# A four-layer hybrid on one core: Mamba's weights and the first group statistics made during layer 0, later norms on ACT, bias tables by chunk

## The chip, the core and the metric

The kernel is one program on 1 core of one Trainium2 chip. Its time is device microseconds of one execution. Five runs of the kernel before took 7926.34 to 7949.28 us, with a median of 7930.91 us. Engines are named as in the profile: PE multiplies matrices (PEld is its weight load), DVE is the vector engine, ACT the scalar engine, POOL the general one, and SP issues the DMAs.

## The reference, cut to what matters

Four images of 56 x 56 positions and 128 channels pass through four layers. Each layer adds its result to x.

```python
def _gn(v, G=32, eps=1e-5): ...     # group norm over all positions and 4 channels of each group

x = x + _L0_conv_ref(_gn(x), ...)   # attention of 4 heads in a 7 x 7 neighbourhood, with a bias
                                    # rpb[head, rel_row, rel_col], softmax, projection
x = x + _L1_conv_ref(_gn(x), ...)   # two Mamba blocks along each row of 56 positions

def _mamba_block(h, in_w, cw, cb, xw, dtw, dtb, A_log, Dp, ow):
    u, res = split(h @ in_w)
    u = silu(causal_conv(u, cw) + cb)          # 4 taps
    dt, Bm, Cm = split(u @ xw)
    delta = softplus(dt @ dtw + dtb)
    A = -exp(A_log)                            # 256 channels x 16 states
    y = selective_scan(u, delta, A, Bm, Cm) + u * Dp
    return y * silu(res) @ ow
```

Layers 2 and 3 (additive attention, experts, softmax attention, a router) are not touched by the change. All is float32.

## The kernel before

x stays in SBUF as four tiles X (112 rows of two image lines, 28 tiles of 128 channels). The work of an image is cut into 7 chunks of 448 positions (8 image lines). On PE, ACT, DVE and POOL the order of instructions in layers 0 to 2 is the order in which the code calls them; the order of SP's DMAs is set by a scheduler, and each DMA of SP also waits until the DMA eight before it is done.

**Group norm** (`group_norm_steps`, L167 to L238). `transposed(c)` turns four tiles of a chunk on PE into a PSUM tile m (L179). `taken(c)` takes its statistics on DVE (`bn_stats`, L190) and copies the chunk unnormed into xnT on ACT (L191), which waits for the statistics; at chunk 0 POOL sets the pad to zero (L188). Six steps follow: aggregate on DVE (L195), mean over the group by a matmul (L199), deviations (L203 to L207), another matmul, variance and ACT's Sqrt (L211, L213), its inverse (L218 to L222). Last, `normed` subtracts the mean and multiplies on DVE in place (L226), seven instructions for an image, called in groups of 2, 2 and 3 chunks. `group_norm_coarse` joins these into twelve steps for layer 0.

**Bias tables** (`bias_tables`, L249 to L300). A table of exp(bias) is made from a constant `toep` (14 x 3136) and the transposed rpb: seven matmuls (L272) and seven ACT exponentials (L276) into one SBUF tile tab, one DMA to a DRAM tile dtab (L279), and 56 DMAs from there into e_edge (42, L285) and e_inner (14, L295), by which the weights of attention are multiplied.

**Layer 0** (`layer0`). SP's order at the start, in the program as built, is: toep, four of rpbT, image 0 in two halves, group, wqkv, bqkv, wproj, bproj, image 1's first half, dtab, image 1's second half, the 56 table DMAs, images 2 and 3. PE's order is: the seven table matmuls, image 0's norm, the first queries, keys and values, scores of the first two units. A chunk is four units, 112 in all. In unit i PE makes the scores of the unit after next (L440) and sums (L470), ACT the exponentials (L450), DVE (three heads) and POOL (one head) the products with the tables (L455); then come the steps that a dictionary `at` holds for this unit: queries (L403, L405), keys, values, the parts of `finish` (copies L485, reciprocal L490, product L491, projection L496, sum into X L499). The twelve norm steps of image b + 1 are spread over units 0 to 16 of image b, so image 3 has none. Layer 0's PSUM pool for m has two buffers.

**Layer 1** (`layer1_weights`, `layer1`, `mamba_pre`). When layer 0 has ended, the weights are loaded and worked: taps times in_proj (L604), A times a pick matrix (L607), D times a unit matrix (L613), columns of x_proj (L601), exp(A_log) on ACT (L596). Then image 0's group norm is done at one go, and the loop over pairs starts. There are 56 blocks (image, chunk, Mamba layer) of 16 pairs. A pair is two matmuls to decays (L671) and inputs (L680), an exponential E on ACT (L696), a product with the inputs on DVE (L701), a scan on DVE (L708) and a product on POOL (L713); PE sums them (L719). The dictionaries `first` and `last` hold what else is done in a pair, before and after its scan: the block's preparation (`mamba_pre`: convolution L826, silu L838, projections L844 and L855, softplus L869, residual L880) one block ahead, and, in the last five blocks before an image starts, that image's transposes, statistics and norms. Layer 1's PSUM pool for m has one buffer.

Of the kernel before, what the change touches and what calls it, by code (L numbers as in the profile page):

```python
# [2 lines left out]

# [16 lines left out]
P = 128  # L20
# [84 lines left out]
class Hybrid:  # L105
# [61 lines left out]
    def group_norm_steps(self, b, pool, psum, group, pad=0):  # L167

        nc = self.nc
        got = {}
        chunk = lambda c: got["xn"][:, c * SEQ : (c + 1) * SEQ, pad:]

        def transposed(c):
            got["ps"] = ps = psum()
            for k in range(TC):
                nc.tensor.transpose(  # L179
                    ps[:, k * TP : (k + 1) * TP], self.X[b][:, TC * c + k, :], self.ident[:TP, :TP]  # L180
                )

        def taken(c):
            if c == 0:
                got["xn"] = self.t(pool, [P, HW, pad + HW], "xnT")
                got["st"] = self.t(pool, [P, NCH, nc.vector.BN_STATS_DIM], "gn_st")
                if pad:
                    nc.gpsimd.memset(got["xn"][:, :, 0:pad], 0.0)  # L188
            ps = got["ps"]
            nc.vector.bn_stats(got["st"][:, c, :], ps[:, :CH])  # L190
            nc.scalar.copy(chunk(c), ps[:, :CH].rearrange("p (s t) -> p s t", t=HW))  # L191

        def aggregate():
            got["mv"] = self.t(pool, [P, 2], "gn_mv")
            nc.vector.bn_aggr(got["mv"], got["st"])  # L195

        def by_group(of):
            got["ps"] = psum()
            nc.tensor.matmul(got["ps"][:, 0:1], group, of(), start=True, stop=True)  # L199

        def mean():
            got["mean"] = mean = self.t(pool, [P, 1], "gn_mean")
            nc.vector.tensor_copy(mean, got["ps"][:, 0:1])  # L203
            got["dev"] = dev = self.t(pool, [P, 1], "gn_dev")
            nc.vector.tensor_sub(dev, got["mv"][:, 0:1], mean)
            nc.vector.tensor_mul(dev, dev, dev)
            nc.vector.tensor_add(dev, dev, got["mv"][:, 1:2])  # L207

        def var():
            got["ve"] = ve = self.t(pool, [P, 1], "gn_ve")  # L210
            nc.vector.tensor_scalar(ve, got["ps"][:, 0:1], 1e-5, None, op0=ALU.add)  # L211
            got["r"] = self.t(pool, [P, 1], "gn_r")
            nc.scalar.activation(got["r"], ve, AF.Sqrt)  # L213

        def root():
            r, ve = got["r"], got["ve"]
            q = self.t(pool, [P, 1], "gn_q")
            nc.vector.reciprocal(r, r)  # L218
            nc.vector.tensor_mul(q, r, r)
            nc.vector.tensor_mul(q, q, ve)  # L220
            nc.vector.tensor_scalar(q, q, -0.5, 1.5, op0=ALU.mult, op1=ALU.add)
            nc.vector.tensor_mul(r, r, q)  # L222

        def normed(cs):
            for c in cs:
                nc.vector.tensor_scalar(  # L226
                    chunk(c), chunk(c), got["mean"], got["r"], op0=ALU.subtract, op1=ALU.mult
                )

        bind = lambda f, c: lambda: f(c)  # L230
        return got, (
            [(bind(transposed, c), bind(taken, c)) for c in range(NCH)],
            [
                aggregate, lambda: by_group(lambda: got["mv"][:, 0:1]), mean,
                lambda: by_group(lambda: got["dev"]), var, root,
            ],
            [bind(normed, cs) for cs in (range(0, 2), range(2, 4), range(4, NCH))],
        )  # L238

    def group_norm_coarse(self, *args):  # L240

        got, (chunks, stats, norms) = self.group_norm_steps(*args)
        both = lambda fs: lambda: [f() for f in fs]
        return got, [both(fs) for fs in chunks] + [both(stats[:3]), both(stats[3:])] + norms
# [4 lines left out]
    def bias_tables(self, pool, tmp, dr, m):  # L249
# [9 lines left out]
        toep = self.load(tmp, [1 + KR, S], "toep", a["k_toep"])  # L259
# [8 lines left out]
        def make():  # L268
            tab = self.t(tmp, [NH * KR, S], "tab")
            for c in range(NCH):  # L270
                ps = m()[: NH * KR]
                nc.tensor.matmul(  # L272
                    ps[:, :CH], rT.rearrange("p h r -> p (h r)"), toep[:, c * CH : (c + 1) * CH],
                    start=True, stop=True,
                )
                nc.scalar.activation(tab[:, c * CH : (c + 1) * CH], ps[:, :CH], AF.Exp)  # L276

            dtab = dr.tile([NH, KR, HW, HW], F32, name="dtab")
            nc.sync.dma_start(out=dtab.rearrange("h r k j -> (h r) (k j)"), in_=tab)  # L279
# [70 lines left out]
    def layer0(self):  # L350
# [5 lines left out]
        with ExitStack() as ctx:  # L356
# [20 lines left out]
            bproj = self.load(wp, [TP, C], "bproj", a["L0_conv_b_proj"].partition_broadcast(TP))  # L377
            for b in range(1, B):
                self.load_image(b)
# [8 lines left out]
            def norm_steps(b):  # L388
                got, steps = self.group_norm_coarse(b, big, m, group)

                def hand_over():
                    steps[-1]()
                    xn[b] = got["xn"].rearrange("p i j -> p (i j)")

                return steps[:-1] + [hand_over]
# [125 lines left out]
            for k, (b, c) in enumerate(chunks):  # L521
# [9 lines left out]
                if c == 0 and b + 1 < B:  # L531
                    for n, step in enumerate(norm_steps(b + 1)):
                        add(i + 3 * n // 2, step)
            scores(0)
# [15 lines left out]
    def layer1_weights(self, wp):  # L550
        nc, a = self.nc, self.a
        w = {}
# [32 lines left out]
        with ExitStack() as ctx:  # L585
            tmp = ctx.enter_context(self.tc.tile_pool(name="l1_tmp", bufs=1))
            iw = self.load(tmp, [P, NL, DI], "iw", in_w[:, :, 0:DI])
            cw = self.t(tmp, [P, NL, DI, DC], "cw")
            nc.sync.dma_start(
                out=cw.rearrange("p l f k -> p (l f k)"),  # L590
                in_=a["L1_conv_conv_w"].rearrange("l f o k -> (l f o k)").partition_broadcast(P),
            )
            A = self.load(
                tmp, [P, NL, NHALF, DS], "A", by_channel("L1_conv_A_log", "l (h p) n -> p l h n")
            )
            nc.scalar.activation(A, A, AF.Exp)  # L596
            xw = self.load(
                tmp, [P, NL, NHALF, DBL], "xw_in", by_channel("L1_conv_x_proj_w", "l (h p) k -> p l h k")
            )
            for at, n, src in ((0, DR, 0), (HD, DR, 0), (2 * HD, DS, DR), (3 * HD, DS, DR + DS)):  # L600
                nc.vector.tensor_copy(w["xw"][:, :, :, at : at + n], xw[:, :, :, src : src + n])  # L601
            for l in range(NL):
                for k in range(DC):
                    nc.vector.tensor_mul(w["in"][:, l, k, :], iw[:, l, :], cw[:, l, :, k])  # L604
                for f in range(NHALF):
                    for q in range(QG):
                        nc.vector.scalar_tensor_tensor(  # L607
                            w["A"][:, l, f, q, :].rearrange("p (j n) -> p j n", n=DS),
                            w["pick"][:, q, :].rearrange("p (j n) -> p j n", n=DS), -1.0,
                            A[:, l, f, :].unsqueeze(1).to_broadcast([P, P // DS, DS]),  # L610
                            op0=ALU.mult, op1=ALU.mult,
                        )
                    nc.vector.tensor_scalar(  # L613
                        w["Dd"][:, l, f, :], self.ident, w["D"][:, l, f : f + 1], None, op0=ALU.mult
                    )
        return w

    def layer1(self):
# [5 lines left out]
        with ExitStack() as ctx:  # L624
            wp = ctx.enter_context(tc.tile_pool(name="l1_w", bufs=1))
            w = self.layer1_weights(wp)
# [21 lines left out]
            def prepare_image(b):  # L648

                got, (chunks, stats, norms) = self.group_norm_steps(b, big, m, w["group"], DC - 1)  # L650

                def hand_over():
                    for c in range(NCH):
                        h[b, c, 0] = got["xn"][:, c * SEQ : (c + 1) * SEQ, :]

                return chunks, stats, norms + [hand_over]
# [117 lines left out]
            for j, block in enumerate(order):  # L774
                at = PAIRS * j
                if j and block[1:] == (0, 0):

                    chunks, stats, norms = prepare_image(block[0])
                    for k, (turn, take) in enumerate(chunks):
                        to = at - (5 - k // 3) * PAIRS + 11 + k % 3  # L780
                        add(last, to, turn)
                        add(first, to + 1, take)
                    to = at - 3 * PAIRS + 12
                    for k, (where, step) in enumerate(zip((first, last) * 3, stats)):
                        add(where, to + k // 2, step)
                    for k, step in enumerate(norms):
# [1038 lines left out]
```

## Time and profile before

| what | us |
|---|---|
| median of five runs | 7930.91 |
| the profiled execution (the slowest of the five) | 7949.28 |
| its span in the profile | 7947.5 |
| busy PE, DVE, ACT, POOL | 6744.0, 6087.7, 5019.8, 2552.0 |
| the start, up to the first product with a bias table (L455) | 42.06 |
| last instruction of layer 0 (L499) starts | 563.64 |
| first convolution of layer 1 (L826) starts | 603.39 |
| first scan of layer 1 (L708) starts | 638.34 |

Times in rows of the timeline count from the span's start. A row has start, duration, engine, line, operation, what it writes and reads, how many, and in brackets how long the engine stood idle before it and what ended that. SPq rows are the issues of DMAs, not the transfers. A table by stage has, after the length, busy time and count of PE, PEld, DVE, ACT and POOL, then the mean granted clock of PE, the share of DMA and GB/s. A row of a line's or group's view has count, and least, median and longest duration in ns.

### The profile page before, as it was taken

The page shows a single profiled execution, that of the slowest core. Times are in us where ns is not written, and L with a number is a line of the kernel's source. Part 1 is how long each engine was busy: PE and PEld are TensorE (multiplying, and loading weights), DVE is VectorE, ACT ScalarE, POOL GpSimd, SP SyncE. Part 2 cuts the span into 40 slices and gives each one's busy share as a digit, 9 for nine tenths or more (in the row PEclk, how much of TensorE's full clock was granted, in tenths as well). Part 3 has the DMA queues.
Part 4 walks back from the last instruction along what each step waited for, and adds up shares of the span by engine and source line. Part 5 has one row for each costly group of instructions (what it writes and reads, how often), then busy time and mean ns, then how long its engine had stood idle before and what let it go on. Part 6 is the DMA issues. An engine that isn't in the chain of part 4 may idle for free.

```text
span 7947.5 us, 105809 instructions
## 1 busy us (share of the span) xinstructions
PE 6744.0 (85%) x41037; PEld 2683.2 (34%) x41037; DVE 6087.7 (77%) x10253; ACT 5019.8 (63%) x4916; POOL 2552.0 (32%) x1909
## 2 busy tenths in 40 slices
PE   8878998998999899977777777777777889999999
PEld 4442333333333333322222222222222344444544
DVE  6777999999999999986877886887787755344434
ACT  4545555555555555537998899899889964333332
POOL 4545776777777677750000000000001000000000
PEclk9989999999999999988999999899899989999999
DMA  2000000000000000000000000000003101210000
GB/s 54 2 14 1 1 1 1 1 1 1 1 1 1 1 1 1 1 5 1 1 1 1 5 1 1 1 5 1 1 28 116 46 6 40 96 56 5 6 5 6
DMA packets 85490, 102.36 MB, mean 13 GB/s; under 512 B 21158, under 2 KB 50742, under 8 KB 84279
## 3 DMA queue, kind: packets, MB, share of 16 engines
q1 hardware_dynamic: 84985, 95.58, 4.1%
q8 instruction: 322, 5.28, 0.3%
q14 instruction: 183, 1.50, 0.1%
HBM read 85.28 MB, written 10.29 MB: 12 GB/s over the span
## 4 chain that ended last, share of the span: by engine, by line
DVE 36%; PE 35%; ACT 20%; issue 7%; POOL 1%; DVEq 0%; DMA 0%; SPq 0%; ACTq 0%; POOLq 0%
DVE hs L708 17%; ACT th L1051 13%; DVE u L701 7%; PE q L1597 7%; PE o L1608 7%; PE s L1062 6%; DVE th L1042 5%; PE o L1089 3%; PE pe L1762 2%; ACT E L696 2%; DVE e L455 2%; PE a L671 2%; PE m L826 1%; DVE d L490 1%; ACT e L450 1%
## 5 line engine op out<-in xcount | busy, mean ns | idle before, releaser
L1051 ACT ACTIVATE th<-th 128x3136 f32<-128x3136 f32 (+12 forms) x1120 | 2294.2, 2093 | 209.2 <-DVE th L1042 155.5
L1042 DVE TENSOR_SCALAR th<-fT,g 128x784 f32<-128x784 f32 (+6 forms) x3920 | 1917.0, 555 | 504.1 <-PE s L1062 467.7
L713 POOL TENSOR_TENSOR hs<-hs,bc 128x896 f32<-128x896 f32 x896 | 1868.2, 2085 | 798.8 <-DVE hs L708 770.6
L1062 PE MATMUL s<-th,place 128*32 128x392 f32 (+8 forms) x14336 | 1497.5, 495 | 668.5 <-ACT th L1051 665.4
L708 DVE TENSOR_TENSOR_SCAN hs<-E,u 128x896 f32<-128x896 f32 x896 | 1809.3, 2019 | 115.7 <-DVE u L701 2.0
L696 ACT ACTIVATE E<-a 128x896 f32<-128x896 f32 x896 | 821.5, 917 | 812.5 <-PE u L680 342.7
L671 PE MATMUL a<-delta,A_pick 32*128 32x448 f32 x3584 | 984.2, 601 | 147.0 <-ACT E L696 138.9
L680 PE MATMUL u<-du,pick 32*128 32x448 f32 x3584 | 981.5, 603 | 47.5 <-DVE hs L708 47.4
L701 DVE TENSOR_TENSOR u<-u,bc 128x896 f32<-128x896 f32 x896 | 963.6, 1075 | 47.2 <-PE u L680 46.9
L1062 PEld LDWEIGHTS s<-th,place 128*32 128x32 f32 (+1 forms) x14336 | 429.3, 111 | 1616.1 <-ACT th L1051 1083.9
L1602 ACT ACTIVATE e<-q,shift 128x448 f32<-128x448 f32 (+1 forms) x700 | 440.7, 633 | 733.1 <-PE q L1597 732.8
L1080 POOL TENSOR_TENSOR e<-e,later 112x112 f32<-112x112 f32 x112 | 80.1, 715 | 2337.7 <-ACT e L1073 1688.5
L1608 PE MATMUL o<-e,xk 128*128 128x448 f32 (+1 forms) x1400 | 654.6, 550 | 25.6 <-ACT oT L1583 25.6
L1767 DVE SCALAR_TENSOR_TENSOR X<-pe,r_gate,X 112x128 f32<-112x128 f32 x896 | 313.8, 350 | 456.2 <-PE pe L1762 420.7
L1597 PE MATMUL q<-xT 128*128 128x448 f32 (+1 forms) x1400 | 655.5, 550 | 6.0 <-ACT e L1602 5.9
L671 PEld LDWEIGHTS a<-delta,A_pick 32*128 32x128 f32 x3584 | 296.2, 188 | 694.7 <-ACT E L696 465.4
L719 PE MATMUL y<-hs,sum 128*32 128x448 f32 x3584 | 445.2, 568 | 4.4 <-POOL hs L713 4.4
L1089 PE MATMUL o<-e,xa 112*128 112x392 f32 (+5 forms) x1024 | 438.8, 552 | 1.1 <-POOL e L1080 1.1
L680 PEld LDWEIGHTS u<-du,pick 32*128 32x128 f32 x3584 | 297.4, 189 | 213.9 <-DVE hs L708 196.1
L1608 PEld LDWEIGHTS o<-e,xk 128*128 128x128 f32 (+1 forms) x1400 | 263.0, 192 | 310.4 <-issue 275.5
L1597 PEld LDWEIGHTS q<-xT 128*128 128x128 f32 (+1 forms) x1400 | 249.1, 190 | 244.0 <-issue 212.1
L1696 POOL MEMSET lc_xa<- 112x4 f32 x28 | 3.1, 109 | 894.8 <-DVE lc_xa L1690 580.1
(251 smaller groups left out, 7226.2 us busy)
## 6 DMA issues: line engine op xcount, KB each, us to landing
wide<-in_L_ffn_weight SPq DMA_DIRECT2D x64, 1024.0 KB
X<-in_x SPq DMA_DIRECT2D x8, 784.0 KB
out<-X SPq DMA_DIRECT2D x28, 224.0 KB
M<-wide SPq DMA_DIRECT2D x4, 784.0 KB
wide<-M SPq DMA_DIRECT2D x4, 784.0 KB
e_edge<-dtab SPq DMA_DIRECT2D x42, 49.0 KB
cw<-in_L_conv_conv_w SPq DMA_DIRECT2D x1, 1024.0 KB
c_h<-in_L_ffn_weight SPq DMA_DIRECT2D x16, 64.0 KB
```

The lines of the kernel that those rows point to most:

```text
L671: nc.tensor.matmul(halves(to)[:, k], w["A"][own, order[j][2], f, q, :], pre[j]["delta"][own, f], start=True, stop=True,)
L680: nc.tensor.matmul(halves(to)[:, k], w["pick"][own, q, :], pre[j]["du"][own, f], start=True, stop=True,)
L696: nc.scalar.activation(E[p + 1], t, AF.Exp)
L701: nc.vector.tensor_mul(v, v, pre[p // PAIRS]["bc"][:, 0:1].to_broadcast([P, 2, CH]))
L708: nc.vector.tensor_tensor_scan(flat, E.pop(p), V.pop(p), 0.0, op0=ALU.mult, op1=ALU.add)
L713: nc.gpsimd.tensor_mul(HS[p], HS[p], bc[:, 1:2].to_broadcast([P, 2, CH]))
L1042: nc.vector.tensor_scalar(th[i][:, blk, lo:hi], fT[j][:, lo:hi], im[order[j][0]]["g"][:, at : at + 1], None, op0=ALU.add,)
L1051: nc.scalar.activation(own, own, AF.Tanh)
L1062: nc.tensor.matmul(ps[j, J][QW * blk : QW * blk + rows, h, lo:hi], place[:, off : off + rows], z[:, blk, h * HALF + lo : h * HALF + hi], s ...
L1089: nc.tensor.matmul(po[j][:, h, lo:hi], im[b]["xa"][:, J, :], e[:, h * HALF + lo : h * HALF + hi], start=(J == 0), stop=(J == t + ((h + 1) ...
L1597: nc.tensor.matmul(ps[:n, :CH], xT[b][:, k : k + n], xT[b][:, c * CH : (c + 1) * CH], start=True, stop=True,)
L1608: nc.tensor.matmul(po[b, c], xk[b][:n, t, :], es.pop((b, c, t))[:n], start=(t == 0), stop=(t == N - 1))
```

## The change

The group norm becomes an object whose parts are called one by one: `place` (the tile xnT and its pad), `turn` (transposes), `stats` (statistics, with no copy), `raw` (ACT's copy), `groups` (the six steps; the last also makes off = -mean * r), `normed` (as before, on DVE) and `scaled`, which is new: one ACT instruction r * x + off per chunk, in place or straight from PSUM.

```diff
+            g.off = self.t(pool, [P, 1], "gn_off")
+            nc.vector.scalar_tensor_tensor(
+                g.off, g.mean, -1.0, g.r, op0=ALU.mult, op1=ALU.mult
+            )
...
+        def scaled(c, of=None):
+            of = g.chunk(c) if of is None else by_row(of[:, :CH])
+            nc.scalar.activation(g.chunk(c), of, AF.Identity, bias=g.off, scale=g.r)
```

The images of layer 0 still use `raw` and `normed`. In layer 0 image 3, which had no norm steps, now carries image 0's transposes, statistics and group steps for layer 1 (`next_norm`, nine steps). The preparation of Mamba's weights becomes a list of 33 steps (1 exponential on ACT; on DVE 4 copies, 4 products of taps, 4 of D, 16 of A, 4 more products of taps), one every second unit from the first unit of chunk 2. The loads are asked for before images 1 to 3; the taps are loaded for one Mamba layer at a time, the second after the first has been used. The pool of these weights now lives from before layer 0.

```diff
+            tmp = ctx.enter_context(tc.tile_pool(name="l1_tmp", bufs=1))
+            next_weights = self.layer1_weights(wp1, tmp)
             for b in range(1, B):
                 self.load_image(b)
...
-                if c == 0 and b + 1 < B:
-                    for n, step in enumerate(norm_steps(b + 1)):
+                if c == 0:
+                    for n, step in enumerate(norm_steps(b + 1) if b + 1 < B else next_norm()):
                         add(i + 3 * n // 2, step)
+            for n, step in enumerate(next_weights):
+                add(first[2] + 2 * n, step)
```

The bias tables are made with two buffers of a chunk each in place of whole tiles; a chunk's toep is loaded and its table stored on its own.

```diff
             for c in range(NCH):
+                own = slice(c * CH, (c + 1) * CH)
+                toep = self.t(tmp, [1 + KR, CH], "toep", bufs=2)
+                nc.sync.dma_start(out=toep, in_=a["k_toep"][:, own])
+                tab = self.t(tmp, [NH * KR, CH], "tab", bufs=2)
                 ps = m()[: NH * KR]
                 nc.tensor.matmul(
-                    ps[:, :CH], rT.rearrange("p h r -> p (h r)"), toep[:, c * CH : (c + 1) * CH],
+                    ps[:, :CH], rT.rearrange("p h r -> p (h r)"), toep,
                     start=True, stop=True,
                 )
-                nc.scalar.activation(tab[:, c * CH : (c + 1) * CH], ps[:, :CH], AF.Exp)
-            dtab = dr.tile([NH, KR, HW, HW], F32, name="dtab")
-            nc.sync.dma_start(out=dtab.rearrange("h r k j -> (h r) (k j)"), in_=tab)
+                nc.scalar.activation(tab, ps[:, :CH], AF.Exp)
+                nc.sync.dma_start(out=flat[:, own], in_=tab)
```

In layer 1 the norms of images 1 to 3 are seven `scaled` in seven successive pairs, where DVE's three groups were. Image 0 has its chunk 0 turned and scaled from PSUM before the loop, and chunks 1 to 6 in the last pairs before the first scan, two to a pair.

```diff
+                        add(last, at - 2 * PAIRS + 3 + c, g.scaled, c)
...
-                    for k, step in enumerate(norms):
-                        add(last, at - 2 * PAIRS + 3 + 2 * k, step)
+                    add(last, at - 2 * PAIRS + 10, hand_over, block[0], g)
...
-            chunks, stats, norms = prepare_image(0)
-            for step in [f for fs in chunks for f in fs] + stats + norms:
-                step()
+            g = self.first_norm
+            g.place(big, DC - 1)
+            hand_over(0, g)
+            for c in range(NCH):
+                turned = lambda c=c: (g.turn(c, m), g.scaled(c, g.ps))
+                if c == 0:
+                    turned()
+                else:
+                    add(last, -PAIRS + 11 + (c - 1) // 2, turned)
```

As built, SP's order at the start becomes: image 0's first half, four of rpbT, image 0's second half, group, wqkv, bqkv, two toep pieces, wproj, bproj and three of Mamba's loads, cb; then loads of toep pieces and stores of table chunks by turns, with dtb, D, pick, sum and dbl_w between them; the 56 table DMAs; one k_state, iw, A, xw_in, cw; images 1, 2 and 3. PE's order at the start is as before, with image 1's first transposes right after the scores of the first two units and the second queries.

## The prediction

> **What bounds the kernel now.** I read the page's slices first, then a table of busy time by stage, then the timeline at the three places that the edits touch, and the chain of waits to see which engine sets the pace there.
>
> ```profile
> PE   8878998998999899977777777777777889999999
> ...
> DVE  6777999999999999986877886887787755344434
> ...
> POOL 4545776777777677750000000000001000000000
> ```
>
> A slice is 199 us. The first three are layer 0, up to about 3560 us is layer 1 (Mamba); the change touches nothing later. The stages:
>
> ```profile
> 45.00:150.00 105.00, 92.62 (x1123) 52.16 (x1125) 77.52 (x97) 52.58 (x73) 57.14 (x50) 0.90 0.18 37
> ...
> 540.00:556.00 16.00, 11.90 (x140) 6.38 (x134) 12.66 (x13) 5.18 (x8) 8.96 (x10) 0.92 0.00 1
> 556.00:600.00 44.00, 10.57 (x62) 6.87 (x54) 18.82 (x48) 5.73 (x11) 0.27 (x1) 0.54 0.19 55
> 600.00:640.00 40.00, 29.34 (x63) 10.91 (x64) 7.31 (x19) 14.35 (x20) 2.22 (x3) 0.73 0.00 0
> ...
> 740.00:1340.00 600.00, 545.69 (x2751) 190.40 (x2752) 571.43 (x397) 334.74 (x408) 430.38 (x247) 0.95 0.00 1
> ```
>
> After the stretch come PE, PEld, DVE, ACT and POOL busy. Layer 0 is shared between PE (88%) and DVE (74%, later up to 87%). In 556 to 640 no engine is full: that is the hand-over from layer 0 to layer 1. In layer 1 DVE is 95% busy and the chain of waits there lies on its scans and products (42% and 18%), so DVE time taken away there counts nearly whole. There are four terms.
>
> **1. The hand-over (gain).**
>
> ```profile
> 563.64 0.69 DVE L499 TENSOR_TENSOR X<-m,X 112x512 f32<-112x512 f32 x1 [1.35 <-PE m L496]
> ...
> 576.29 2.17 DVE L604 TENSOR_TENSOR in_w<-iw,cw 128x256 f32<-128x256 f32 x4 [6.53 <-DMA cw<-in_L_conv_conv_w]
> ...
> 585.48 1.01 PE L179 MATMUL m<-ident,X 112*128 112x112 f32 x4 [21.95 <-ACT xnT L191]
> ...
> 603.39 5.60 PE L826 MATMUL m<-xnT,in_w 128*128 128x448 f32 x8 [2.09 <-DVE xnT L226]
> ```
>
> Layer 0 ends at 563.6. Then come the loads of weights (to 576.3), their products on DVE (to 584), seven rounds of transpose, statistics and copy of 2.30 us each (to 598.7), group statistics and norms, and the first convolution at 603.39. After the change weights and statistics are there, and chunk 0's transpose already stands ahead of PE's last projections, as it does now; so the first convolution can follow PE's last projection at 563.5: 39.9 us earlier. Chunks 1 to 6 are still turned and scaled before the first scan, one after the other, because layer 1 has one PSUM buffer m: transposes 1.01, scaling from PSUM like L834's ACTIVATE (bias, 128x448) 0.63 or a little more, two hand-overs of 0.05: about 1.8 each, 10.9 for six. ACT's first exponential, now at 633.23, waits behind them. Term: -39.9 + 10.9 = **-29.0**, of which I take **-28.5** (the new copy of chunk 0 may wait for a buffer of layer 0); bounds -31 and -24.
>
> **2. Norms of images 1 to 3 in layer 1 (gain).**
>
> ```profile
> 1270.28 2.67 DVE L226 TENSOR_SCALAR xnT<-xnT,gn_mean,gn_r 128x448 f32<-128x448 f32 x2
> 1270.51 2.20 POOL L713 TENSOR_TENSOR hs<-hs,bc 128x896 f32<-128x896 f32 x1 [1.40 <-DVE hs L708]
> ...
> 1288.06 3.09 DVE L226 TENSOR_SCALAR xnT<-xnT,gn_mean,gn_r 128x448 f32<-128x448 f32 x3
> ```
>
> Seven norms cost DVE 2.67 + 2.67 + 3.09 = 8.4 us per image: the first of each group ends only when POOL's L713 does (2.27 us at most, against 0.49 alone). They go to ACT, three images: -25.3. Each image adds one small DVE operation (gn_off) at 0.2 (0.16 and its gap; up to 1.95, the row of gn_q in layer 1, if it meets POOL): +0.6. ACT gets 7 x 0.63 = 4.4 us per image in seven pairs of 3.14 us. ACT is not idle there: in the same phase of an ordinary block (1107 to 1123, silu and softplus with their table loads) it waits about 3 us in all, but its exponentials are done 2.7 us or more ahead of their scans. Five of the seven fall there (3.1 us); I charge 0.4 per image, +1.2. Term: **-23** (-25 to -11: at the far end all 13.2 us of ACT show). The queue behind a scaling on ACT is the next exponential E, for which DVE's scan waits.
>
> [...]
>
> **3. The start (loss).**
>
> ```profile
> 5.40 10.66 PE L272 MATMUL m<-toep,rpbT 14*52 14x448 f32 x14 [5.40 <-DMA rpbT<-in_L_conv_rpb]
> ...
> 21.87 10.27 SPq L285 DMA_DIRECT2D e_edge<-dtab  x21
> ...
> 45.45 0.95 PE L179 MATMUL m<-ident,X 112*128 112x112 f32 x4
> ...
> 49.30 8.04 SPq L126 DMA_DIRECT2D X<-in_x  x4
> ```
>
> Now the table matmuls run 5.40 to 16.06, the norm of image 0 follows on PE, and the 56 table DMAs are issued by SP from 21.87 to 49.30 (27.4 us). Image 1 was issued at 9.54 and 17.03, so its first transposes at 45.45 never wait. In the program as built SP's order is another: image 0, rpbT, group, wqkv and bqkv, the first two toep pieces, then five of Mamba's loads, loads and stores of the table by turns with more weights between them, the 56 table DMAs, one k_state, iw, A, xw_in, cw, and only then image 1.
> First toep piece: image 0 (1568 KB), group and wqkv (256 KB) are ahead in the rings; at 0.24 MB/us from 2 us on they end near 9.6; with 2 us to land, 11.6. A round of a buffer (two chunks): issue 0.5, landing 2.2 (D, issued to 566.66, used at 568.88), matmul 1.52: 4.2. Seven chunks end at 11.6 + 1.5 + 3 x 4.2 = 25.7, 9.7 later than now; all of PE's start moves with it. The last store lands near 29.0 (now 21.87), the 56 issues end at 56.4, five more at 0.49 at 58.9. Ahead of image 1's first half (784 KB) stand 880 KB of iw, A, xw_in and cw: 1.66 MB at 0.245 from 57.5 on is 6.8: it lands near 65. PE stands in order at its transposes from 55.3 to 65, 19.5 later than 45.45. I take back 1.5: DVE has caught up meanwhile, and the 3.17 us that ACT's copy at 47.99 now waits for statistics shrinks. Term: **+18**; bounds +10 (everything caught up but the PE shift) and +34 (a round of 9.5: with the store's 4.9 us, the row 16.99 to 21.87, in the same round).
>
> [...]
>
> **4. New steps in layer 0 (loss).**
>
> ```profile
> 224.11:248.72 24.61, 18.08 (x224) 10.88 (x216) 17.86 (x27) 9.95 (x15) 12.90 (x11) 0.86 0.01 1
> ...
> 480.83:496.69 15.86, 14.80 (x216) 8.60 (x212) 13.78 (x16) 8.97 (x13) 9.14 (x10) 1.00 0.01 2
> ```
>
> One chunk of image 1 (with norm steps) against one of image 3 (without). Over its first five chunks image 1 takes 103.0, image 3 79.8: twelve norm steps with 9.9 us of DVE cost 23.2. Most of it is order, not work: ACT's copies stand 26.8 us behind statistics (178 to 270), PE stands 5.2 at L199 for the aggregate. Image 3 now gets nine such steps without the copies and norms. PE +7 x 0.55 in chunks where it is 93% busy, one stand at L199 (about 4 after slack), ACT's Sqrt with two table loads of 1.28: **+9** (3 to 23).
> The weights are 33 steps, one every second unit, one of them on ACT (0.26). DVE: 0.45 + 0.87 + 4.33 + 3.38 = 9.0 us at the hand-over's rows. In a chunk without norm steps DVE waits 0.5 and 1.5 us for ACT, just after the places of these steps; about ten of the 33 fall among norm steps, where no such gap is. **+4** (0 to 21, which is 9.0 x 23.2/9.9). Four gn_off, 0.2 each: +0.8. Term: **+13.8**. The copies of weights need no wait: all have landed by 65, the second cw is asked for after the last product of layer 0's taps and used forty units later. POOL's queue gets nothing but the memsets that it had.
>
> **Sum.** -28.5 - 23 + 18 + 13.8 = -19.7. The profiled execution is the slowest of the five, 7949.28 with a span of 7947.5; it becomes 7929.6. Against the median, 7930.91 - 19.7 = **7911**.
>
> **Rivals.**
> - The start costs its far end: rounds of 9.5 instead of 4.2, +16: 7927. For: the stores share SP's queue with the loads and weights. Against: loads stand two ahead of their stores. 0.15.
> - ACT becomes the bound where the scalings stand: term 2 falls to -11: 7923. For: its table loads leave 3 us of gaps. Against: the lead of 2.7. 0.10.
> - Less loss: the weights hide whole, image 3's steps cost 3 and the start 10, nothing shows on ACT: -28.5 - 24.7 + 10 + 3.8 = -39: 7892. For: DVE's gaps. 0.17.
> - **Slower:** layer 0 charges by hand-over, not by work. Twelve steps cost 23.2, 1.93 each; 42 new ones at that price are 81 instead of 13: 7979. It ends slower from 0.80 per step on (33.5/42), and measurably from 1.2. For: chunks of image 1. Against: DVE's gaps lie where the steps are put, and only 16 of the 42 are like norm steps. 0.12.
> - The change doesn't do what it says: the first convolution still waits for something else near 590 to 600, term 1 vanishes: 7939. Against: nothing else stands in PE's order. 0.04.
>
> **Numbers.** The forecast has 0.42, about 7903 to 7919. A change within 0.2% (15.9 us) is about what a measurement here can't tell from none; faster means below 7915.0. Of the forecast's 0.42 0.30 lie there, of the quick case 0.17, of the others 0.04: faster 0.51; slower 0.11; same 0.38. The range 7891 to 7934 leaves out the slow case and the idle one, and some edges.
>
> **What would show it.** First convolution near 564 plus the start's and layer 0's delay, and six transposes with scalings just ahead of the first exponential; no DVE L226-like groups in layer 1, scans at 3.14 through those pairs; PE's table matmuls ending near 26, its first transposes of image 1 near 65 with a wait for that load; image 3's first chunks some 2 us longer each, with a stand at the aggregate. I am wrong if image 1 lands much after 65, or if chunks of images 0 to 2 grow by over 1 us per weight step.

## The result and the profile after

The changed kernel took 7930.18 us in the median of 25 runs (7920.98 to 7936.43), beside 7932.03 for 45 runs of the kernel before: a ratio of 0.9994 (95% interval 0.9988 to 0.9999). A second set of runs, on another chip, gave 7921.95 against 7938.62, 0.9977 (0.9968 to 0.9985). The forecast, 7911, was 19 us too low in the first set and 11 in the second; the range held both times. The profiled executions show more than the first ratio does: 7927.72 with a span of 7925.9, against 7949.28 and 7947.5.

The page's slices after, PE, DVE and POOL: the first is emptier (the start), the rest reads as before.

```profile
PE   7888989998999899977777777777777889999999
...
DVE  6787999999999999986877786887787755344434
...
POOL 4455777777777777750000000000001000000000
```

The stages of every profile taken, in us. "3rd query" is the third `q<-m,bqkv` on DVE, where image 1's load has shown its price; "layer 0 ends" is the start of its last addition to X; "behind" runs from the last scan to the span's end. No instruction differs there. Runs below the line are told further down; each ratio goes by the runs of the kernel before on the same chip. b_rep, a_rep, e_norms and e_x1mid stood on one chip, e_start, e_root, e_best and e_hand on a second, e_x1mid2, e_start2 and e_spread on a third, e_late on a fourth. The changed kernel was run in the first set and on the first of these chips only, so a run on the others is compared with it by ratios, and it has two of them, 0.9994 and 0.9977.

| kernel | 3rd query | layer 0 ends | to first scan | first to last scan | behind | median | ratio |
|---|---|---|---|---|---|---|---|
| before | 66.6 | 563.6 | 74.7 | 2896.3 | 4412.8 | 7932.0 | 1 |
| before, again (b_rep) | 64.2 | 560.9 | 78.0 | 2893.4 | 4403.3 | 7937.0 | 0.9996 (0.9988–1.0005) |
| changed | 87.8 | 598.9 | 47.5 | 2871.4 | 4408.1 | 7930.2 | 0.9994 (0.9988–0.9999) |
| changed, again (a_rep) | 87.1 | 601.0 | 47.5 | 2873.5 | 4399.2 | 7922.0 | 0.9977 (0.9968–0.9985) |
| --- | | | | | | | |
| e_norms | 64.7 | 561.8 | 76.4 | 2869.6 | 4400.3 | 7908.0 | 0.9961 (0.9949–0.9972) |
| e_x1mid | 78.0 | 590.6 | 47.3 | 2869.1 | 4400.2 | 7921.3 | 0.9975 (0.9965–0.9985) |
| e_x1mid2 | 77.5 | 590.4 | 47.2 | 2869.1 | 4396.6 | 7907.0 | 0.9964 (0.9951–0.9976) |
| e_start | 64.7 | 576.7 | 47.8 | 2871.3 | 4401.8 | 7896.1 | 0.9948 (0.9936–0.9961) |
| e_start2 | 64.7 | 576.7 | 47.7 | 2869.3 | 4396.9 | 7894.8 | 0.9950 (0.9938–0.9963) |
| e_root | 87.5 | 592.7 | 49.7 | 2870.3 | 4402.6 | 7917.2 | 0.9977 (0.9967–0.9987) |
| e_best | 67.1 | 571.7 | 51.5 | 2876.0 | 4404.2 | 7899.8 | 0.9954 (0.9940–0.9968) |
| e_hand | 64.4 | 569.0 | 48.2 | 2903.2 | 4387.1 | 7913.0 | 0.9973 (0.9964–0.9982) |
| e_spread | 66.5 | 571.0 | 38.7 | 2868.4 | 4387.2 | 7867.1 | 0.9920 (0.9906–0.9933) |
| e_late | 86.1 | 601.2 | 37.7 | 2869.3 | 4396.0 | 7912.9 | 0.9976 (0.9966–0.9985) |

In the first pair of profiles the touched stages give +35.3 in layer 0, -27.3 in the hand-over and -24.9 in layer 1: -16.9. In the second pair they give +40.2, -30.6 and -19.8: -10.2.

**The start.** The timeline of the changed kernel:

```profile
22.54 1.70 PE L284 MATMUL m<-toep,rpbT 14*52 14x448 f32 x2 [0.38 <-DMA toep<-in_k_toep]
24.18 1.75 PE L184 MATMUL m<-ident,X 112*128 112x112 f32 x8
...
55.36 20.13 SPq L127 DMA_DIRECT2D X<-in_x  x6
...
65.45 0.98 PE L184 MATMUL m<-ident,X 112*128 112x112 f32 x4 [13.77 <-DMA X<-in_x]
```

The table matmuls end at 24.24 instead of 16.06. SP asks for image 1 only at 55.36, behind the 56 table DMAs and the weights. PE stands 13.77 us, in order, at the transposes of an image that it needs for later work.

**The hand-over**, in the timeline of the changed kernel:

```profile
598.94 0.69 DVE L531 TENSOR_TENSOR X<-m,X 112x512 f32<-112x512 f32 x1 [1.35 <-PE m L528]
...
599.83 5.24 PE L882 MATMUL m<-xnT,in_w 128*128 128x448 f32 x8 [0.99 <-POOL xnT L178]
...
628.10 1.01 PE L184 MATMUL m<-ident,X 112*128 112x112 f32 x4 [0.62 <-ACT raw_res L944]
629.15 0.73 ACT L247 ACTIVATE xnT<-m,gn_off,gn_r 128x448 f32<-128x448 f32 x1 [1.10 <-PE m L184]
629.92 1.01 PE L184 MATMUL m<-ident,X 112*128 112x112 f32 x4 [0.82 <-ACT xnT L247]
...
638.28 0.73 ACT L247 ACTIVATE xnT<-m,gn_off,gn_r 128x448 f32<-128x448 f32 x1 [1.10 <-PE m L184]
...
646.39 2.02 DVE L755 TENSOR_TENSOR_SCAN hs<-E,u 128x896 f32<-128x896 f32 x1
```

The first convolution follows the layer's last addition by 0.89 us, where it took 39.75. Then PE and ACT wait for each other through six rounds, 1.83 us from transposes to transposes, and DVE does nothing until 645.19.

**The norm of image 1 in layer 1**, the changed kernel's rows of ACT and DVE:

```profile
1275.90 0.78 ACT L247 ACTIVATE xnT<-xnT,gn_off,gn_r 128x448 f32<-128x448 f32 x1
...
1277.78 0.78 ACT L247 ACTIVATE xnT<-xnT,gn_off,gn_r 128x448 f32<-128x448 f32 x1
```

```profile
1275.23 2.02 DVE L755 TENSOR_TENSOR_SCAN hs<-E,u 128x896 f32<-128x896 f32 x1
1277.16 1.07 DVE L748 TENSOR_TENSOR u<-u,bc 128x896 f32<-128x896 f32 x1
1278.37 2.02 DVE L755 TENSOR_TENSOR_SCAN hs<-E,u 128x896 f32<-128x896 f32 x1
```

Scans stay 3.14 apart where DVE's groups of 2.67 and 3.09 stood between them, but for one. The tenth interval of the block is 4.53 us, where the same interval of the next block is 3.74:

```profile
1289.55 3.42 PE L799 MATMUL m<-ow,yg 128*112 128x128 f32 x16
...
1294.23 1.10 DVE L748 TENSOR_TENSOR u<-u,bc 128x896 f32<-128x896 f32 x1 [0.53 <-PE u L727]
```

DVE stands 0.53 for PE, whose sixteen products before took 3.42 us at a granted clock of 0.56; in the next block they take 2.00 at 1.00 (from 1340.44), and DVE does not stand. Images 2 and 3 have the same interval at 4.55 and 4.52. So the norms of an image still cost some 0.8 us, 2.4 in all. That it is the scalings on ACT which set PE back is not shown; the kernel before, with its norms on DVE, has 3.74 there.

**Image 3**, whose third chunk carries the group statistics, in the changed kernel:

```profile
516.62 0.33 DVE L201 BATCH_NORM_AGGREGATE gn_mv<-gn_st 128x2 f32<-128x42 f32 x1
517.10 0.35 PE L205 MATMUL m<-gn_mv,group 128*128 128x1 f32 x2 [3.67 <-DVE gn_mv L201]
...
529.99 0.86 PE L502 MATMUL o<-e,v 112*32 112x392 f32 x8 [1.44 <-ACT oT L517]
```

PE stands 3.67 us for an aggregate that waits in DVE's queue behind products of the bias table, and again 1.44 behind ACT's square root. From query to query this chunk takes 22.6 us (508.68 to 531.31), against 15.9 before.

### The profile page after: what moved, and what is told of

Same layout as the page of the kernel before. It is cut to its first block, busy times and chain, and to the rows that moved or that the text cites. A ratio compares the mean times of both kernels' runs of the same rounds, so it can differ in the third digit from the quotient of the medians.

```text
span 7925.9 us, 105871 instructions
## 1 busy us (share of the span) xinstructions
PE 6723.6 (85%) x41065; PEld 2676.0 (34%) x41065; DVE 6065.3 (77%) x10233; ACT 5034.0 (64%) x4938; POOL 2552.0 (32%) x1909
## 4 chain that ended last, share of the span: by engine, by line
DVE 35%; PE 35%; ACT 20%; issue 7%; POOL 1%; DVEq 0%; DMA 0%; SPq 0%; ACTq 0%; POOLq 0%
DVE hs L755 18%; ACT th L1107 13%; DVE u L748 7%; PE q L1653 7%; PE o L1664 7%; PE s L1118 6%; DVE th L1098 5%; PE o L1145 3%; PE pe L1818 2%; ACT E L743 2%; DVE e L487 2%; PE a L718 2%; PE m L882 1%; DVE d L522 1%; ACT e L482 1%
## 5 line engine op out<-in xcount | busy, mean ns | idle before, releaser
L1118 PE MATMUL s<-th,place 128*32 128x392 f32 (+7 forms) x14336 | 1502.9, 497 | 669.5 <-ACT th L1107 666.6
```

The source lines that it names most:

```text
L1118: nc.tensor.matmul(ps[j, J][QW * blk : QW * blk + rows, h, lo:hi], place[:, off : off + rows], z[:, blk, h * HALF + lo : h * HALF + hi], s ...
```

## The experiments

Theory S: the four terms are there and add up, and a difference of some 10 us hides in what differs from run to run. Rival V: what a stage gains is given back elsewhere, by a later wait or by PE's clock.

### Both kernels again (b_rep, a_rep)

> The kernel before once more, for a second trace. Theory S (the stages add up): layer 0 ends near 563.6, the first scan starts near 638.3 and the last near 3534.7, as in the first trace, and the run's distance from 7949 lies in what comes after the last scan (4413 there). Theory V (a touched stage varies from run to run): one of the first three numbers moves by 10 us or more. Its ratio to before: 1.000.

> The changed kernel once more, for a second trace. Theory S: layer 0 ends near 598.9, first scan near 646.4, last scan near 3517.8, and only what comes after the last scan (4408) differs. Theory V: one of the first three moves by 10 us or more. Ratio to before 0.9994 as in the first measurement if that was no accident, 0.998 if the sum of stages holds.

The kernel before again: 0.9996 of itself. The changed kernel: 0.9977, 17 us (interval 12 to 25), where the two sums of stages are 16.9 and 10.2. The first set's interval, 1 to 10 us, lies below both. No stage up to the last scan moved by 10 us between the two traces of a kernel, so theory S holds for the stages; for the median of the first set it does not. The two sets differ by 8 us for one and the same changed kernel, and by 7 us for the one before, in the other direction. That is the scale below which no single ratio here says anything.

### The norms of images 1 to 3 alone (e_norms)

```diff
+            nc.scalar.activation(chunk(c), chunk(c), AF.Identity, bias=got["off"], scale=got["r"])
...
-                    for k, step in enumerate(norms):
-                        add(last, at - 2 * PAIRS + 3 + 2 * k, step)
+                    for c in range(NCH):
+                        add(last, at - 2 * PAIRS + 3 + c, got["scaled"], c)
```

> The kernel before with one part of the change alone: the norms of images 1 to 3 in layer 1 as seven ACT instructions each, in the changed kernel's places. Theory S: layer 1 is 23 to 25 us shorter, a block with norms takes 51.7 in place of 59.6, and the time falls by as much, ratio 0.997. Rival (the gain is given back later, since what follows layer 1 gets longer or other blocks do): trace of the norm blocks the same, but the ratio at 0.999 or above.

Layer 1 takes 2869.6, 23.8 less than the kernel before in this set, and the ratio is 0.9961: 30.6 us, interval 22 to 40. Term 2 is confirmed alone, nothing is given back later, and this edit by itself beats the whole change.

### Image 1 asked for earlier (e_x1mid, e_x1mid2)

```diff
+                self.load_image(1)
...
-            for b in range(1, B):
+            for b in range(2, B):
                 self.load_image(b)
```

The new line stands in make, behind the loop over chunks. As built, SP issues image 1 right behind the first two toep pieces.

> The changed kernel with one edit: image 1 is asked for before the table DMAs and Mamba's weights. Theory (the start's loss is 8 us of PE shift and 11 to 13 of waiting for image 1): image 1's first transposes stand near 57 in place of 65, since some of the table's loads now queue behind image 1; the time falls by 7 to 9 us against the changed kernel. Rival (the stand is made good later in layer 0 anyway): transposes near 57, but layer 0 ends within 3 us of 598.9.

```profile
53.59 0.68 DVE L488 TENSOR_TENSOR e<-e,e_edge 112x504 f32<-112x504 f32 x1 [3.20 <-DMA e_edge<-dtab]
...
55.35 0.55 PE L184 MATMUL m<-ident,X 112*128 112x112 f32 x4
```

In this timeline image 1's transposes at 55.35 wait for nothing, and layer 0 ends 10.4 us sooner than in a_rep. The first product with the table, at 53.59, comes 13.8 later than in b_rep (39.77): here the tables are what is late. The median, however, was that of the changed kernel, so the run was made again.

> The run with image 1 loaded earlier, again: its layer 0 ended 10 us sooner than the changed kernel's, but its median did not show it (7921.3; eight runs from 7909 to 7931). Theory S: the gain is there and the eight runs were an uneven draw; the ratio comes out at 0.9958 to 0.9970. Rival V (the granted clock gives it back): 0.9973 to 0.9985 again.

Up to the last scan the stages were the same to 0.5 us, and the median was 7906.95, 0.9964, where S has it. The two intervals (0.9965 to 0.9985 and 0.9951 to 0.9976) overlap. Of the first eight runs the three at a mean granted clock of 0.950 or 0.951 took 7909 to 7916 us, the five at 0.944 to 0.947 took 7921 to 7931, so V is not excluded for the first draw.

### The start of the kernel before (e_start, e_start2)

```diff
+        whole = lambda n: self.t(big, [P, HW, HW], "xnT").rearrange("p i j -> p (i j)")[:n]
+        toep = whole(1 + KR)
+        nc.sync.dma_start(out=toep, in_=a["k_toep"])
...
+            tab = whole(NH * KR)
...
-            tmp = ctx.enter_context(tc.tile_pool(name="l1_tmp", bufs=1))
-            next_weights = self.layer1_weights(wp1, tmp)
             for b in range(1, B):
                 self.load_image(b)
+            tmp = ctx.enter_context(tc.tile_pool(name="l1_tmp", bufs=1))
+            next_weights = self.layer1_weights(wp1, tmp)
```

Nothing has to be cut into chunks: the buffers of xnT are empty while the tables are made.

> The changed kernel with the start of the kernel before: the table and the Toeplitz matrix whole, in the two buffers that images 0 and 1 take for their norms later, and Mamba's loads behind all four images. So far layer 0 ended at 599 to 601 in the changed kernel, at 561 to 564 in the one before, and of the 35 to 40 between them 21 to 23 were there at the third query of image 0 (66 against 88). Theory S (the stages add up): the third query comes back to 64 to 67, layer 0 ends at 577 to 580, nothing else moves, and the time falls by 20 to 23 against the changed kernel of this chip: a ratio of 0.9945 to 0.9955. Rival V (what layer 0 gains is given back by the granted clock in later stages): the run with image 1 loaded earlier ended layer 0 10.4 us sooner and had the median of the changed kernel all the same (7921.3 against 7922.0); then this one too stays within 8 us of it, 0.9967 or more, with layer 0's end at 578.

```profile
39.93 0.68 DVE L488 TENSOR_TENSOR e<-e,e_edge 112x504 f32<-112x504 f32 x1 [3.20 <-DMA e_inner<-dtab]
...
43.32 0.95 PE L184 MATMUL m<-ident,X 112*128 112x112 f32 x4
```

The start is that of the kernel before (39.77 and 43.06 in b_rep), layer 0 ends at 576.7, 22 to 24 sooner, and the ratio falls to 0.9948. The repeat stood beside other kernels on another chip:

> The run with the start of the kernel before, again, beside the others on this chip. Theory S: a ratio of 0.9942 to 0.9955 as the first time (0.9948), layer 0 ending at 574 to 580. Rival V: 0.9960 or more. Its profile also says how far the stages of one and the same kernel differ between runs: layer 0's end, hand-over, layer 1 and the rest by up to 3, 4, 3 and 10 us if the spread is what the other runs show.

0.9950, all stages within 5 us of the first time. So the start costs the changed kernel 22 to 24 us of layer 0. Against its ratio of 0.9977 the whole of it shows (21 to 23 us), against 0.9994 it would be 35 to 37; the changed kernel was not run on these two chips. The edit makes two mends at once, the tables whole and Mamba's loads behind the images, and what each gives alone was not tried.

### The group statistics cut finer (e_root), and with the start (e_best)

```diff
                 chunk = lambda c: lambda: (g.turn(c, m), g.stats(c))
-                return [chunk(c) for c in range(NCH)] + [both(parts[:3]), both(parts[3:])]
+                return [chunk(c) for c in range(NCH)] + parts[:3], parts[3:]
...
+                    for step in late:
+                        add(len(units) + 3, step)
```

> The changed kernel with the group statistics of the first image cut finer: the aggregate a unit ahead of the product that needs it, the small operations a unit behind that, and the square root with its two table loads after layer 0's last exponential. In the changed kernel image 3's third chunk takes 22.6 us where it took 15.9 before, with PE standing 3.67 for the aggregate and 1.44 behind the square root. Theory S: the chunk falls to 16 to 17.5, layer 0 ends 5 to 7 sooner than at 599 to 601, and the time falls by as much, to a ratio of 0.9968 to 0.9972. Rival: the 9.5 us of image 3 are the seven turns and statistics in DVE's and PE's queues, wherever the rest stands; then layer 0 ends within 2 us of 600.

```profile
516.33 0.33 DVE L201 BATCH_NORM_AGGREGATE gn_mv<-gn_st 128x2 f32<-128x42 f32 x1
...
521.83 0.38 PE L205 MATMUL m<-gn_mv,group 128*128 128x1 f32 x2
524.62 0.67 DVE L436 TENSOR_SCALAR q<-m,bqkv 128x448 f32<-128x448 f32 x1
```

PE no longer stands for the aggregate and the chunk takes 16.2 us (508.39 to 524.62). Layer 0 ends 6.2 to 8.3 sooner, but the hand-over takes 2.3 longer: 4 to 6 us are left at the first scan. The square root and its small operations now stand just ahead of layer 0's last addition, yet the first convolution follows that addition by 1.14 us, against 0.89. The rest lies behind it. From layer 0's end to the first scan in the changed kernel and in e_root (after the length: busy PE, PEld, DVE, ACT, POOL, granted clock, DMA):

```profile
598.94:646.39 47.45, 33.94 (x76) 13.83 (x76) 1.79 (x2) 17.75 (x23) 2.49 (x4) 0.66 0.00 0
```

```profile
592.73:642.45 49.72, 35.67 (x76) 14.01 (x76) 1.79 (x4) 17.75 (x23) 2.46 (x4) 0.62 0.00 0
```

The same 76 matmuls took 1.7 us longer at a lower clock, 0.62 against 0.66. The ratio, 0.9977, is outside the 0.9968 to 0.9972 of S and can't show so little.

> Both mends together: the start of the kernel before, and the finer group statistics. Theory S: layer 0 ends at 570 to 574, 28 sooner than in the changed kernel, the hand-over to the first scan takes 47 to 49, layer 1 the 2869 to 2874 of the kernels with norms on ACT, and the time is 27 to 30 below the changed kernel's: a ratio of 0.9937 to 0.9945, some 12 to 16 us below the run that only moved the norms (0.9961). Rival V: the clock gives it back, and the time is not below that of the run that only moved the norms.

0.9954, not below e_start on the same chip (7899.8 against 7896.1): layer 0 ends 5.1 sooner than there, but the hand-over takes 3.7 and layer 1 4.7 longer. The expected 27 to 30 became 18 by the ratios, against 0.9977, and below e_norms (0.9961) it is 6 us with overlapping intervals, not 12 to 16. So S missed, and V is not excluded: in time the mend of the statistics is not shown to be worth anything. The next run shows that most of the 3.7 is not of the edit.

### The hand-over alone (e_hand)

```diff
-                        add(last, at - 2 * PAIRS + 3 + c, g.scaled, c)
+                    for k, cs in enumerate((range(0, 2), range(2, 4), range(4, NCH))):
+                        add(last, at - 2 * PAIRS + 3 + 2 * k, g.normed, cs)
```

> The run with both mends, but the norms of images 1 to 3 in layer 1 on DVE again, in three groups as in the kernel before: the hand-over alone. Theory S (the parts add): layer 0 ends and the first scan starts as in the run with both mends; layer 1 takes 2893 to 2896 again, 23 to 26 more; the ratio is 0.9967 to 0.9975. Rival: the parts don't add (the norms on ACT gain only because DVE's phase moved): layer 1 is then within 8 us of the 2869 to 2874.

The ratio, 0.9973, is where S has it, and the rival is excluded. Layer 1 takes 2903.2, 27 more than in e_best and above the 2893 to 2896 of S; that it is also 7 to 10 longer than in the kernel before stays unexplained. The medians differ by only 13 us; in the traces e_hand's stretch behind layer 1, where no instruction differs, is 17 shorter. Up to the first scan this kernel and e_best are one and the same program. Two stretches show what a run can change by itself, again from layer 0's end to the first scan. First e_hand, then e_best:

```profile
568.99:617.23 48.24, 34.48 (x76) 14.12 (x76) 1.79 (x4) 17.77 (x23) 2.47 (x4) 0.65 0.00 1
```

```profile
571.65:623.16 51.51, 37.73 (x76) 15.10 (x76) 1.79 (x3) 17.77 (x23) 2.48 (x4) 0.58 0.00 0
```

The same 76 matmuls take 34.48 us at a granted clock of 0.65 and 37.73 at 0.58, and the stage is 3.3 longer.

### Five of the six rounds put into layer 1 (e_spread, e_late)

```diff
-                    add(last, -PAIRS + 11 + (c - 1) // 2, turned)
+                    add(last, PAIRS * (c - 2) + 11, turned)
```

Chunks 4 to 6 are not used before block 8, and chunk 2 not before block 2; only chunk 1 has to be ready. First on top of e_best:

> The run with both mends, and of the six rounds of turning and scaling ahead of the first scan only that of chunk 1 stays there; chunks 2 to 6 are turned and scaled during the blocks of layer 1, each a block ahead of its use. Theory S (the rounds are a price of the hand-over that stands wholly on the path): the first scan comes five rounds of 1.83 sooner, 9 us, at 608 to 615 (the two runs with this layer 0 had 617 and 623), layer 1 takes 2871 to 2880, and the time is 5 to 12 below 7899.8, the median of the run with both mends: a ratio of 0.9940 to 0.9950. Rival (the rounds only move): each turn and scaling holds PE, PSUM and ACT in layer 1, which gives back 1 to 2 us a piece; layer 1 then takes 9 us more and the ratio stays within 0.0006 of 0.9954.

7867.13, 0.9920: the fastest kernel of the study. The first scan comes at 609.7, as S has it, and layer 1 gives nothing back, 2868.4. But 33 us below e_best, which stood on another chip, is more than five rounds, and the ratio is below the 0.9940 to 0.9950 of S. Of the 38 us between the two profiled executions 17 lie behind layer 1. Then the same line alone, on the changed kernel:

> The changed kernel as it is, with that one edit alone: chunks 2 to 6 of the first image turned and scaled during layer 1. In the run with the mends the edit went with 33 us (7867 against 7900), of which the traces put 7.5 to 13.5 before the first scan, 7.6 in layer 1 and 17 behind layer 1, where no instruction differs and where another kernel without the edit also had the short 4387 us. Theory S (the edit is worth its five rounds; the rest is the granted clock of that run, half speed in 174 us of a stretch behind layer 1 where others had 184 to 218): the first scan comes at 637 to 640 instead of 646 to 648.5, hand-over 37 to 40 instead of 47.5, and the ratio is 0.9960 to 0.9970 (the changed kernel: 0.9977 and 0.9994). Rival (the edit itself shortens what follows, 20 us and more): 0.9950 or less, with 4387 us behind layer 1 again.

```profile
601.20:638.90 37.70, 28.27 (x56) 10.42 (x56) 1.79 (x2) 14.12 (x18) 2.50 (x4) 0.71 0.00 0
```

The stage from layer 0's end to the first scan falls from 47.5 to 37.7: 9.8 us for five rounds of 1.83 and a little clock (0.71 against 0.66). The median, 7912.9, is 9 to 17 us below the changed kernel's two medians, but it stood on another chip, and the ratio, 0.9976, misses the 0.9960 to 0.9970 of S and is not below 0.9977. Behind layer 1 stand 4396.0. So the edit is worth its 9 us up to the first scan in the trace, and the time does not show them; the rival's 0.9950 is excluded, and what more e_spread gained is not shown to be the edit's.

## Why the prediction was right and where it was off

**What bounds the kernel:** held. DVE's time in layer 1 counted nearly whole (23.9 of 25.3 us), and layer 0 charged for order (PE's stands of 13.77, 3.67 and 1.44).

**1. Hand-over, forecast -28.5 (-39.9 + 10.9, taken as -28.5):** -27.3. The convolution came 38.9 nearer (39.75 to 0.89 behind layer 0), and from it to the first scan the time grew by 11.6 (34.95 to 46.56), of which six rounds of 1.83 are 11.0. In the second pair it is -30.6, since the kernel before had 78.0 there with the same code.

**2. Norms on ACT, forecast -23:** the three blocks with a norm lost 8.67, 7.46 and 7.81 us, 23.9 together. e_norms has 23.8 for layer 1. One reading was wrong: not the first norm of each group but the second ends with POOL's L713 (in the first group 0.49 us from 1270.28, then 2.27 from 1270.69); the group's time, and so the term, is the same. A scaling took 0.747 to 0.780 us in SBUF, not the 0.63 that I charged. The exponentials stayed 2.5 us or more ahead of their scans in these blocks; the 2.4 us of the tenth intervals stand against the 1.2 that I charged for ACT. DVE was the full engine there, 95% busy from 740 to 1340 in the kernel before, where ACT was 56%.

**3. Start, forecast +18:** +21.2 at the third query, +19.3 at image 1's first, and 22.9 and 24.4 in the second pair; e_start puts it at 22 to 24 whole. The landing was forecast at 65 and came at 65.45; the first toep piece was forecast at 11.6 and used at 11.90. What was mis-sized is the 1.5 taken back for DVE and ACT catching up: nothing of it came by the third query, and from the transposes to that query 1.2 more were lost (22.3 against 21.1). The rounds of the table took 3.5 to 3.6 us (11.90, 15.36, 18.97, 22.54), below the 4.2 of the forecast and far from the rival's 9.5. I had also put PE's arrival at the transposes at 55.3; it came at 51.7, so PE stood 13.8 and not 9.7.

**4. New steps, forecast +13.8:** from image 1's first query to layer 0's end the first pair differs by 16.0: images 1 and 2 by 6.2 together, image 3 by 9.8 (forecast 9). In this pair the weights are what was mis-sized, 4 for 33 steps against 6.2 for the 25 in images 1 and 2. That is 0.25 us a step; the slower rival needed 0.80 and priced 1.93. In e_start, with the same steps, images 1 and 2 grow by 3.6 only. And e_start, which has the new steps but the old start, ends layer 0 13.1 and 15.9 us after the two traces of the kernel before, so the term stands as a whole. The stand at the aggregate was forecast at 4 and was 3.67.

**The sum:** -19.7 forecast, -16.9 and -10.2 in the two pairs of traces. **The step that failed is the last one:** "Against the median, 7930.91 - 19.7 = 7911". The first set's medians differ by 1.85, the second's by 16.7. A difference between two executions was carried over to medians whose single runs lie 26 us apart, taken from the slowest of five at that. The profiled execution itself was forecast at 7929.6 and took 7927.7, but this owes something to luck: of its 21.6 us below the one before, 4.7 lie behind layer 1, where nothing was changed.

**Range and chances:** the range held both medians because it was wide. The 7903 to 7919 to which the forecast gave 0.42 held neither, and a time below 7915.0, to which all cases together gave 0.51, did not come in either set.

**Rivals:** ACT as the bound, the slower hand-over price and the change that does nothing are excluded by scans at 3.14, 0.25 us a step, and the convolution at 599.83. The quick case is excluded by layer 0's 16 us. Of the signs named for each step all but one came: 599.83 (564 plus 35.8), six rounds ahead of the first exponential at 640.32, no DVE norms in layer 1, tables ending at 24.24, image 1 at 65.45, the stand in image 3. Image 3's chunks did not grow by some 2 us each: the second, third and fourth grew by 1.7, 0.6 and 6.8, so most of the price is the one chunk with the group statistics.

**Open:** why the changed kernel's median was 7930 on one chip and 7922 on the other. That the stretches of PE's clock, told below, fell differently is argued, not shown: only one execution of each set has a trace. The mean granted clocks of the changed kernel's runs, 0.9464 and 0.9472, account for some 3 of the 8 us, an estimate from the 3.0 and 3.6 us by which runs of one set differ per 0.001 of clock.

## What to carry to other kernels

A change with two gains and two losses is best taken apart: here the one edit on the full engine (norms off DVE) was worth more alone than all four together, and the larger loss came from the cut of the tables and the loads put ahead of image 1. Before a load is cut into pieces to free memory, look for buffers that are empty at that time, and put loads that are needed 500 us later behind those that PE's next instruction in order waits for. Work that a hand-over must not contain is found by asking when each piece is first read: five of six rounds were needed a block or more later.

## What the runs showed of the hardware

The record of PE's granted clock in the traces of the kernel before and the changed one has two levels, 1.0 and 0.5 of full speed. But for the last, where the record ends, its stretches are multiples of 3.413 us to within 1 ns (in the kernel before 109 of 316 are one, 60 are two; in the changed kernel 84 and 60 of 284), and they do not begin at the same instant in the two: counted from the span's start, 0.58 us behind a multiple in the one, 3.10 in the other. Half speed lasted 912 us of the kernel before's profile, 864 and 837 of the changed kernel's two, 758 of e_spread's. The length of the stretch behind layer 1, in which all kernels are alike, goes with it:

| kernel | half speed behind layer 1 | length |
|---|---|---|
| before | 540 us | 4412.8 us |
| changed | 536 us | 4408.1 us |
| e_best | 520 us | 4404.2 us |
| changed, again | 509 us | 4399.2 us |
| e_hand | 485 us | 4387.1 us |
| e_spread | 479 us | 4387.2 us |

The other eight profiles have 492 to 520 us of half speed there and lengths of 4396.0 to 4403.3. A line through all fourteen has some 0.4 us of length for each us of half speed, an estimate; the table alone does not say which of the two makes the other. In the table of a stretch the same shows in the granted clock. From 1000 us behind the last scan to 2471 us behind it, in the kernel before and in e_spread:

```profile
4534.68:6005.68 1471.00, 1097.55 (x8501) 381.41 (x8494) 1148.46 (x2628) 1325.15 (x814) 52.17 (x75) 0.93 0.03 9
```

```profile
4478.10:5949.10 1471.00, 1093.19 (x8572) 379.07 (x8575) 1158.38 (x2646) 1339.64 (x823) 53.74 (x79) 0.94 0.03 9
```

More instructions fit into the same 1471 us, 8572 matmuls against 8501, at 0.94 against 0.93. The runs without a trace say the same: of 26 runs of the kernel before on one chip, the two at a mean clock of 0.941 had spans of 7952 and 7954, the three at 0.946 or 0.947 had 7926 to 7933. The 25.7 us between 4387.1 and 4412.8 are 0.3% of the time, more than the change moved in either set of runs. What makes PE cross into half speed at a given place was not tried.
